# A residual term moved from an elementwise add into TensorE's sum, with a rewritten opening, in an edge-gated graph kernel

## The chip, the cores and the metric

The kernel runs on one core of one Trainium2 chip. The metric is the device time of one execution in microseconds (us). Of the kernel before there are three runs, with a median of 1230.34 us.

## What is computed

There are B = 16 batches of C = 1024 nodes with D = 256 features. Both `A_a` and `A_m` are the same sparse matrix `adj` (a few entries per row, and the diagonal).

```python
pre_u = einsum('bud,dk->buk', h_t, W1[:d]);  pre_v = einsum('bvd,dk->bvk', h_t, W1[d:])
hidden = relu(pre_u[:, :, None, :] + pre_v[:, None, :, :] + b1)
S = sigmoid(einsum('buvk,ko->buvo', hidden, W2)[..., 0] + b2[0])
a_t = einsum('buv,bud->bvd', S * A_a, h_t)
m_t = einsum('uv,bud->bvd', A_m, h_t) * h_t
z_t = beta1 * h_t + beta2 * (a_t @ Wa + ba) + beta3 * (m_t @ Wm + bm)
```

The change concerns the first term of the last line, `beta1 * h_t`. All of it is fp32.

## The kernel before, in words

**Blocks and steps.** The work is cut into 32 blocks: 4 groups of 4 batches (`GB`) times 8 tiles of 128 nodes. A block has 10 steps, so the main loop (L679) has 320 steps; s is the step within a block. In each step one list of 128 edges is handled. `fetch` (L450, POOL) gathers 128 rows of 8 KB from a table in DRAM: the left half of a row is pre_u, the right half is h. `expand` (L519, TensorE, two steps ahead) repeats the target rows pre_v into PSUM, in the two buffers `pc`. `gate` (L537) runs on VectorE: one add of table row and `pc` (L540), then four multiply-and-sum instructions (L544); then on ScalarE the sigmoid (L547) and four scalings (L550), followed by `left_adj` (L534) for the next step. `aggregate` (L552, TensorE, one step behind) sums the gathered h rows into PSUM by 32-column matmuls. Five gather buffers (`fetched`) are in turn.

**End of a block.** The sums are copied out (`half_end`, L569, ScalarE), transposed by TensorE and copied again by ScalarE (`turn_over`, L579 and L582), and half of them multiplied by hT on VectorE (`times_h`, L592). `block_end` (L597) forms the output in steps 3 to 6 of the next block: for each half of the batches a bias row (L382), then per batch two matmuls with `w_m` and two with `w_a` (L609), each with 128x128 stationary values and 256 moving columns, into a PSUM tile of two batches. In steps 5 and 7, after the gate of that step, VectorE does `h_blk = h_blk * beta1 + pz` (L613), where `h_blk` holds the rows of h, loaded from DRAM on SP's queue in the block's step 4 (L708). SP then writes `h_blk` out (L616). `tail` (L630) does the same in pieces for the last block.

**Other work between.** `rows` (L385) computes pre_u for the table of a group ahead of its use, `halves` (L403) pre_v of the next block. `load_hT` (L364, SP) loads transposed h for both, into a rotation of 10 buffers; a block's hT is freed after `times_h`. All small sums (`p`, `pl`, `pt`, `pz`) share two PSUM buffers, `misc`. `lists` (L241) is a generator in 11 pieces that makes the edge lists of one tile of nodes out of a loaded row block of adj (`key`); the heavy pieces are three maxima over 1024 columns on VectorE. Its calls are spread over the first 100 steps by the table `advance` (L660), and `fetch_val` gathers the edge values, on POOL.

**Order.** The kernel is scheduled by hand: each engine and each queue runs its instructions in the order in which the code issues them. `after(step, f)` puts a piece into a later step, where `do(n)` (L430, L694) issues it: after that step's gate and ahead of its `block_end`, `turn_over` and `halves`.

**The opening** (L458 to L501). POOL loads the keys of lists 0 to 3 (three of them into gather buffers) and clears the gather buffers. SP loads eight hT and copies rows of h into the table. Then a script of 15 strings orders `rows` (r), pieces of lists 0, 1 and 2 (digits), the value gathers (v), halves of block 0 (h) and the first five gathers (f). List 3 goes on in steps 4 to 17.

Of the kernel before, what the change touches and what calls it, by code (L numbers as in the profile page):

```python
# [13 lines left out]
P = 128  # L14
# [3 lines left out]
def kernel(  # L18
# [17 lines left out]
    out: bass.AP,  # L36
):


# [58 lines left out]

    w_u = load_weights(W1[0:D], "w_u")
    b1_b = load_rows(b1, D, "b1_b")  # L100
    w_v = load_weights(W1[D:2 * D], "w_v")
    w2_b = load_rows(W2, D, "w2_b")
# [4 lines left out]


    ones = fixed([P, 2], "ones")
    nc.vector.memset(ones[:, 0:1], 1.0)  # L110
# [71 lines left out]
    ident = fixed([P, P], "ident")  # L182
    nc.vector.tensor_scalar(ident, upto[:, :P], row, None, ALU.is_equal)
    place = upto[:, :W].rearrange("p (q v) -> p q v", v=V)
    slot, nth = upto, upto[:, :S]
# [11 lines left out]

    b1_p = fixed([P, D], "b1_p", FR)
    bias_p = fixed([P, D], "bias_p", FR)

# [14 lines left out]
    big = main.enter_context(tc.tile_pool(name="big", bufs=2))  # L215
    hts = main.enter_context(tc.tile_pool(name="hts", bufs=NT + 2))
    wk = main.enter_context(tc.tile_pool(name="wk", bufs=3))
# [8 lines left out]
    def aside(vt):  # L226
        return psc.tile([P, GD], FP, name="pc") if vt < EARLY else small("pl")

    NF = 5
    EARLY = 3
    fetched = []
    for i in range(NF):
        fetched.append(gat.tile([P, 2 * GD], FP, name=f"fetched{i}"))

    def clear(i):
        nc.gpsimd.memset(fetched[i][:, N if 1 <= i <= EARLY else 0:], 0.0)


    def lists(vt):  # L241
        key = fetched[vt + 1][:, :N] if vt < EARLY else big.tile([P, N], FP, name="key", bufs=1)
        nc.gpsimd.dma_start(key, adjT[vt * P:(vt + 1) * P, :])
        yield
# [124 lines left out]

    def copy_h(k, engine=nc.scalar):  # L370
        g, nt = k
        engine.dma_start(table[g][nt * P:(nt + 1) * P, GD:].rearrange("n (b d) -> n b d", b=GB),
                            x_rows[nt * P:(nt + 1) * P, g * GB:(g + 1) * GB, :])
# [29 lines left out]
    def halves(k):  # L403
# [13 lines left out]
        for h in range(2):  # L417
# [4 lines left out]
            for w in range(NW):  # L422
                s = slice((1 - w) * W, (2 - w) * W)
                nc.scalar.copy(X[s, w, c], pl[s])  # L424

    engines = mybir.EngineType
    main.enter_context(tc.manual_schedule(
# [13 lines left out]
    T = TW * NW  # L441

    BS = NG * NT

    def where(n):
        k, s = divmod(n, T)
        w, j = divmod(s, TW)
        return k, *order[k], w, j

    def fetch(n):  # L450
# [7 lines left out]
    made = [lists(vt) for vt in range(NT)]  # L458
    turn = [order[i] for i in (*range(2 * NT // 2, 3 * NT // 2), *range(NT // 2))]
    turn += [(1, vt) for _, vt in turn]  # L460
    for i in range(2):
        next(made[i])
    for i in range(NT):
        load_hT(turn[i])
    for i in range(NF):
        clear(i)
    for i in range(2, EARLY + 1):
        next(made[i])
    COPIES = 2
    for i in range(COPIES):  # L470
        copy_h(turn[i], nc.sync)

    script = ("r r 0 0", "r r 0", "r r 0 1", "0 r 1", "0 0 r r", "0 r 1", "r 0 0 v 1 r", "1 r 2 2", "1 1 r r h",
              "1 r h 2", "1 1 h 2", "2 f h h", "2 2", "2", "2 2")
    m = 0
    piece = None
    parts = halves(0)
    for t, turns_ in enumerate(script):
        step = t - 100
        do(step)  # L480
        for c in turns_.split():
            if c == "r":
                if m % 2 == 0:
                    piece = rows(turn[m // 2])
                    next(piece)
                go(piece, step)
                if m % 2 == 0 and m // 2 + COPIES < NT:
                    copy_h(turn[m // 2 + COPIES], nc.sync)
                m += 1
            elif c == "h":  # L490
                go(parts, step)
            elif c == "v":
                fetch_val(T)
                spread(b1_p, b1_b)
                next(parts)
            elif c == "f":
                for n in range(NF):
                    fetch(n)
            else:
                next(made[int(c)], None)  # L500
    do(len(script) - 100)  # L501

    def scale_late():
        nc.vector.tensor_scalar(ba_b, ba_b, be2, None, ALU.mult)
        nc.vector.scalar_tensor_tensor(bias, bias, be3, ba_b, ALU.mult, ALU.add)
        spread(bias_p, bias)
        nc.vector.tensor_scalar(w_a, w_a, be2, None, ALU.mult)
        nc.vector.tensor_scalar(w_m, w_m, be3, None, ALU.mult)

    marks, pcs, accs, evs, hbs, LTs, lefts = {}, {}, {}, {}, {}, {}, {}

# [56 lines left out]
    def turn_over(k, w, q, step):  # L571
# [18 lines left out]
        def times_h():  # L590
            m = LT[:, :, :, 0, v]
            nc.vector.tensor_tensor(m, m, hTs[order[k]].rearrange("p b c n -> p c b n")[:, :, :, v], ALU.mult)  # L592
            if w == NW - 1 and q == 1:
                del hTs[order[k]]
        after(step + 1, times_h)

    def block_end(k):  # L597

        g, vt = order[k]
        hb = hbs[k]  # L600
        for h in range(2):
            for bb in range(2):
                step = yield
                if bb == 0:
                    pz = small("pz")
                    add_row(pz, bias_p)
                for i, wt in enumerate((w_m, w_a)):
                    for c in range(DC):
                        nc.tensor.matmul(pz[:, bb * D:(bb + 1) * D], LTs[k][:, c, 2 * h + bb, i, :], wt[:, c, :],  # L609
                                         start=False, stop=(i == 1 and c == DC - 1), skip_group_check=True)  # L610

            def add(h=h, pz=pz):
                nc.vector.scalar_tensor_tensor(hb[:, 2 * h:2 * h + 2, :], hb[:, 2 * h:2 * h + 2, :], be1,  # L613
                                               pz.rearrange("p (b d) -> p b d", b=2), ALU.mult, ALU.add)
            after(step + 1, add)
        after(step + 2, lambda: nc.sync.dma_start(  # L616
            out[g * GB:(g + 1) * GB, vt * P:(vt + 1) * P, :].rearrange("b p d -> p b d"), hb))
        del hbs[k], LTs[k]

    tails = [(0, W, 0), (0, W, 1), (W, U, 2), (W + U, U, 3)]

    def tail_rows(t, v, m, f):
        g, vt = order[BS - 1]
        for i in range(P // m):
            b = g * GB + i + (f * P // m if m == W else 0)
            yield hbs[BS - 1][i * m:(i + 1) * m, f, :], t[b, vt * P + v:vt * P + v + m, :]

    def tail(parts, step):  # L630

        LT, hb = LTs[BS - 1], hbs[BS - 1]
        v, m, f = parts[0]
# [3 lines left out]
        nc.tensor.matmul(pz[:, :n], unit, bias_p.unsqueeze(1).to_broadcast([P, len(parts), D]),  # L637
                         start=True, stop=False, skip_group_check=True)
        for i, wt in enumerate((w_m, w_a)):
            for r in range(len(parts)):  # L640
# [8 lines left out]
        def add():  # L649
            z = hb[:, f:f + len(parts), :]  # L650
            nc.vector.scalar_tensor_tensor(z, z, be1, pz[:, :n].rearrange("p (r d) -> p r d", d=D), ALU.mult, ALU.add)  # L651
            for part in parts:
                for i, (z, o) in enumerate(tail_rows(out, *part)):
                    (nc.scalar if i % 2 else nc.sync).dma_start(o, z)
# [4 lines left out]

    advance = {}  # L660
    for i in range(EARLY, NT):
        for o in (0, 4, 5, 6, 7, 8, 9, 11, 13, 15, 17)[i == EARLY:]:
            advance[20 * (i - EARLY) + o] = (i,)
    loads = dict(zip((0, 1, 2, 6, 9, 13, 17, 23), turn[NT:]))
# [10 lines left out]
    for n in range(2):  # L675
        expand(n)
    left_adj(0)
    total = BS * T
    for n in range(total + 2):  # L679
# [15 lines left out]
        if n == 1:  # L695
# [7 lines left out]
            after(10, scale_late)  # L703
        if s == 4 and k < BS:
            hbs[k] = big.tile([P, GB, D], FP, name="h_blk")
            if k < BS - 1:
                g, vt = order[k]
                nc.sync.dma_start(hbs[k], x_rows[vt * P:(vt + 1) * P, g * GB:(g + 1) * GB, :])  # L708
            else:
                for v, m, f in tails:  # L710
                    for h, o in tail_rows(x, v, m, f):
                        nc.sync.dma_start(h, o)
        for i in advance.get(n, ()):
# [43 lines left out]
    do(total + 2)  # L757
    assert not due and not hTs and all(next(x, None) is None for x in made)
    main.close()
# [111 lines left out]
```

## Time and profile before

| | |
|---|---|
| median of three runs | 1230.34 us (1225.94 to 1235.77) |
| profiled execution, and its span | 1230.34 us, 1228.5 us |
| mean granted TensorE clock | 0.968 |
| first gate (L540) starts at | 89.16 us |
| blocks 0 to 9 (table of group 1, lists 2 to 7) | 89 to 491 us, 40.2 us each |
| blocks 10 to 14 (rows of group 2) | 491 to 655 us, 32.8 us each |
| blocks 15 and 16 (no rows) | 655 to 720 us, 32.5 us each |
| blocks 17 to 23 (rows of group 3) | 720 to 958 us, 34.0 us each |
| blocks 24 to 31 (no rows) | 958 to 1207 us, 31.1 us each |
| DMA moved | 393.5 MB, of which 31 loads of h_blk of 512 KB |

The starts of the blocks are those of every tenth L540. "Busy" of an engine is the time in which it has an instruction. TensorE overlaps its matmuls, and their ends are modelled, so its rate is read from the distance of starts. PEld is TensorE's loading of stationary values. A wait is put down to the instruction that came last by the profile.

### The profile page before, as it was taken

The numbers are of one execution on the slowest core, as the hardware profiler recorded it, in microseconds if no ns is written. First come the engines' busy times: TensorE is split into PE (matmuls) and PEld (weight loads), VectorE is DVE, ScalarE is ACT, GpSimd is POOL, SyncE is SP. The second block draws the span as 40 slices with busy tenths as digits, with TensorE's granted clock in tenths as the row PEclk, the third lists the DMA queues.
The fourth block names the chain that finished last, engine by engine and source line by source line (L and its number), as shares of the span: only waits on it lengthen the run. The fifth ranks groups of instructions, "written<-read, shape, count | busy, mean of one in ns | idle before, by whom it ended". The sixth has DMA issues, their size and how long they took to land. (4 is left out here: it accounts for less than half of the span.)

```text
span 1228.5 us, 23863 instructions
## 1 busy us (share of the span) xinstructions
PE 1108.6 (90%) x7697; PEld 723.5 (59%) x7697; DVE 1094.8 (89%) x3437; ACT 841.1 (68%) x2562; POOL 425.5 (35%) x419
## 2 busy tenths in 40 slices
PE   4767998997979989999999999999999999999996
PEld 3654665654546555666666556666666555665553
DVE  7659888999999899999899999889888999999994
ACT  1236675775656757777777777777777777777763
POOL 2227362362623614422333323222222333333330
PEclk8768999999999989999999999999999999999998
DMA  9569898898898989999999999999999988999992
GB/s 295 181 245 360 282 349 305 284 334 284 259 331 297 327 291 343 350 358 361 348 362 368 337 347 318 345 345 405 386 354 335 345 320 315 325 339 326 325 334 95
DMA packets 151975, 393.50 MB, mean 320 GB/s; under 512 B 16816, under 2 KB 110512, under 8 KB 115632
## 3 DMA queue, kind: packets, MB, share of 16 engines
q0 software_dynamic: 49792, 300.90, 66.4%
q1 hardware_dynamic: 85488, 76.03, 19.3%
q10 hardware_dynamic: 16560, 14.95, 3.7%
q8 instruction: 63, 1.03, 0.3%
q14 instruction: 72, 0.59, 0.1%
HBM read 395.88 MB, written 50.33 MB: 363 GB/s over the span
## 5 line engine op out<-in xcount | busy, mean ns | idle before, releaser
L452 POOL DMA_INDIRECT fetched<-table,uidx x320 | 329.9, 1031 | 705.0 <-PE acc L561 493.6
L544 DVE SCALAR_TENSOR_TENSOR t<-t,w_b 128x256 f32<-128x256 f32 x1280 | 469.9, 422 | 19.3 <-ACT X L412 0.5
L540 DVE TENSOR_TENSOR t<-fetched,pc 128x1024 f32<-128x1024 f32 x320 | 389.0, 1216 | 50.3 <-PE pc L524 25.2
L561 PE MATMUL acc<-fetched,left 128*32 128x256 f32 x4096 | 323.7, 392 | 26.9 <-ACT left L550 25.7
L550 ACT ACTIVATE left<-left,gt 128x32 f32<-128x32 f32 (+1 forms) x1280 | 299.4, 304 | 10.4
L524 PE MATMUL pc<-X,mark 128*128 128x512 f32 x640 | 247.3, 468 | 3.4 <-DVE t L540 1.9
L561 PEld LDWEIGHTS acc<-fetched,left 128*32 128x32 f32 x4096 | 122.7, 109 | 193.4 <-issue 68.0
L547 ACT ACTIVATE gt<-sc,b_b 128x4 f32<-128x4 f32 x320 | 95.4, 298 | 190.0 <-DVE t L544 189.5
L378 PE MATMUL misc<-w_u,hT 128*128 128x256 f32 x512 | 131.6, 406 | 23.5 <-ACT tab L394 12.9
L609 PE MATMUL misc<-w_m,LT 128*128 128x256 f32 x496 | 133.7, 392 | 0.0
L524 PEld LDWEIGHTS pc<-X,mark 128*128 128x128 f32 x640 | 118.4, 193 | 25.1 <-DVE LT L592 4.1
L609 PE MATMUL misc<-w_a,LT 128*128 128x256 f32 x496 | 127.3, 379 | 0.0
L378 PEld LDWEIGHTS misc<-w_u,hT 128*128 128x128 f32 x512 | 99.3, 202 | 45.1 <-ACT tab L394 14.4
L378 PE MATMUL misc<-w_v,hT 128*128 128x256 f32 x512 | 123.0, 384 | 0.0
L534 ACT ACTIVATE left<-onehot,val 128x128 f32<-128x128 bf16 (+1 forms) x320 | 116.6, 364 | 0.0
L609 PEld LDWEIGHTS misc<-w_m,LT 128*128 128x128 f32 x496 | 88.9, 189 | 34.8 <-issue 25.5
L336 POOL DMA_INDIRECT val<-in_adjT_dram,vidx x80 | 84.0, 1050 | 66.8 <-DVE b_p L194 40.0
L378 PEld LDWEIGHTS misc<-w_v,hT 128*128 128x128 f32 x512 | 98.5, 192 | 13.4
L544 DVE DVE_READ_ACCUMULATOR t<-t,w_b 128x1 f32 x1280 | 104.0, 81 | 0.0
L609 PEld LDWEIGHTS misc<-w_a,LT 128*128 128x128 f32 x496 | 94.2, 190 | 12.8
L569 ACT COPY ev<-acc 128x512 f32<-128x512 f32 x128 | 74.8, 585 | 28.9 <-PE acc L561 28.9
L424 ACT CAST X<-misc 64x512 fp32r<-64x512 f32 x128 | 74.3, 581 | 28.0 <-PE misc L421 23.9
(138 smaller groups left out, 860.1 us busy)
## 6 DMA issues: line engine op xcount, KB each, us to landing
hT<-in_xT_dram SPq DMA_DIRECT2D x40, 512.0 KB, 11.1
table<-tab SPq DMA_DIRECT2D x32, 512.0 KB, 5.2
h_blk<-in_x_dram SPq DMA_DIRECT2D x31, 512.0 KB, 13.4
out_dram<-h_blk SPq DMA_DIRECT2D x31, 512.0 KB, 5.5
table<-in_x_dram ACTq DMA_DIRECT2D x24, 512.0 KB, 11.8
fetched<-table,uidx POOLq DMA_INDIRECT x320, 7.9
table<-in_x_dram SPq DMA_DIRECT2D x8, 512.0 KB, 8.0
key<-in_adjT_dram POOLq DMA_DIRECT2D x5, 512.0 KB, 9.2
```

Source lines behind the costliest of these rows:

```text
L336: nc.gpsimd.indirect_dma_start(out=val[:, i, j:j + 1], out_offset=None, in_=adj_flat, in_offset=bass.IndirectOffsetOnAxis(ap=vidx[:, i, j: ...
L378: nc.tensor.matmul(p[:, bb * D:(bb + 1) * D], hT[:, 2 * h + bb, i, :], wt[:, i, :], start=(i == 0 and not begun), stop=(i == DC - 1), skip ...
L452: nc.gpsimd.indirect_dma_start(out=fetched[n % NF], out_offset=None, in_=table[g], in_offset=bass.IndirectOffsetOnAxis(ap=uidx[:, vt * NW ...
L524: nc.tensor.matmul(pcs[n][:, c], marks[n // TW][:, j * P:(j + 1) * P], cuts[k][:, w, c], start=True, stop=True)
L534: nc.scalar.activation(lefts[n][:, :m, :, 0, :], onehot[:, i, o:o + m, :].unsqueeze(2).to_broadcast([P, m, GB, V]), AF.Copy, scale=val[:, ...
L540: nc.vector.tensor_tensor(t, fetched[n % NF][:, :GD].rearrange("p (b d) -> p b d", b=GB), pcs.pop(n).rearrange("p (b d) -> p b d", b=GB), ...
L544: nc.vector.scalar_tensor_tensor(t[:, b, :], t[:, b, :], 0.0, w2_b, ALU.max, ALU.mult, accum_out=sc[:, b:b + 1])
L547: nc.scalar.activation(gt, sc, AF.Sigmoid, bias=b2_b)
L550: nc.scalar.activation(lefts[n][:, :m, b, 1, :], lefts[n][:, :m, b, 0, :], AF.Copy, scale=gt[:, b:b + 1])
L561: nc.tensor.matmul(accs[h][b * 2 * V:(b + 1) * 2 * V, r, :], left[:, i, b].rearrange("p k v -> p (k v)"), f[:, GD + b * D:GD + (b + 1) * D ...
L569: nc.scalar.copy(evs[q], accs.pop(q))
L609: nc.tensor.matmul(pz[:, bb * D:(bb + 1) * D], LTs[k][:, c, 2 * h + bb, i, :], wt[:, c, :], start=False, stop=(i == 1 and c == DC - 1), sk ...
```

## The change

The term beta1 h becomes two more matmuls per batch in `block_end`: stationary hT (128 features x 128 nodes), moving a 128x128 diagonal `diag` that holds beta1, made once. The finished sum is copied from PSUM by ScalarE into a new tile `z_blk` (one buffer), which SP writes out. Rows of h are no longer loaded. A block's hT is freed at the end of `block_end`, and the rotation has 11 buffers. The tail has the matmuls too, and VectorE copies its sums out.

The opening is another one. The keys of lists 0 and 1 are loaded first on SP, ahead of the eight hT; those of lists 2 and 3 on POOL in the opening's step 5; all into two `key` buffers. ScalarE, not POOL, clears the gather buffers. ScalarE's queue makes the eight copies into the table, each ahead of its `rows`. Ten steps replace the script: lists 0 and 1 advance in each, lists 2 and 3 by five pieces in steps 5 to 9 (in each step ahead of 0 and 1), two halves of `rows` per step. Value gathers come in step 9, the first five gathers after the opening; lists 2 and 3 end in steps 0 to 10 of the main loop. The spread of b1 is done before all lists.

```diff
+    diag = fixed([P, P], "diag")
+    spread(b1_p, b1_b)
-    hts = main.enter_context(tc.tile_pool(name="hts", bufs=NT + 2))
+    hts = main.enter_context(tc.tile_pool(name="hts", bufs=NT + 3))
-        key = fetched[vt + 1][:, :N] if vt < EARLY else big.tile([P, N], FP, name="key", bufs=1)
-        nc.gpsimd.dma_start(key, adjT[vt * P:(vt + 1) * P, :])
+        key = big.tile([P, N], FP, name="key", bufs=2)
+        (nc.sync if vt < 2 else nc.gpsimd).dma_start(key, adjT[vt * P:(vt + 1) * P, :])
+    def clear(i):
+        nc.scalar.copy(fetched[i], zero.to_broadcast([P, 2 * GD]))
...
+    for t in range(1, 11):
+        step = t - 100
+        do(step)
+        for i in (2, 3, 0, 1):
+            if i < 2 or 5 <= t < 10:
+                next(made[i], None)
+        while m < t * OP // 8 and m < OP:
+            if m % 2 == 0:
+                copy_h(turn[m // 2])
+                piece = rows(turn[m // 2])
+                next(piece)
+            go(piece, step)
+            if m % 3 == 0 and m // 3 < NF:
+                clear(m // 3)
+            m += 1
+        if t in (7, 8, 9, 10):
+            if t == 7:
+                parts = halves(0)
+                next(parts)
+            go(parts, step)
+            if t == 10:
+                go(parts, step)
+        if t == 9:
+            fetch_val(T)
...
+        nc.vector.tensor_scalar(diag, ident, be1, None, ALU.mult)
...
     def block_end(k):
         g, vt = order[k]
-        hb = hbs[k]
+        hT = hTs[order[k]]
+        zb = big.tile([P, GB, D], FP, name="z_blk", bufs=1)
...
                     add_row(pz, bias_p)
+                for c in range(DC):
+                    nc.tensor.matmul(pz[:, bb * D + c * P:bb * D + (c + 1) * P], hT[:, 2 * h + bb, c, :], diag,
+                                     start=False, stop=False, skip_group_check=True)
                 for i, wt in enumerate((w_m, w_a)):
...
             def add(h=h, pz=pz):
-                nc.vector.scalar_tensor_tensor(hb[:, 2 * h:2 * h + 2, :], hb[:, 2 * h:2 * h + 2, :], be1,
-                                               pz.rearrange("p (b d) -> p b d", b=2), ALU.mult, ALU.add)
+                nc.scalar.copy(zb[:, 2 * h:2 * h + 2, :].rearrange("p b d -> p (b d)"), pz)
             after(step + 1, add)
...
     def tail(parts, step):
...
+        for r in range(len(parts)):
+            for d in range(DC):
+                for b in range(c):
+                    nc.tensor.matmul(pz[b * m:(b + 1) * m, r * D + d * P:r * D + (d + 1) * P],
+                                     hT[:, r * c + b, d, v:v + m], diag, start=False, stop=False, skip_group_check=True)
...
-            z = hb[:, f:f + len(parts), :]
-            nc.vector.scalar_tensor_tensor(z, z, be1, pz[:, :n].rearrange("p (r d) -> p r d", d=D), ALU.mult, ALU.add)
+            nc.vector.tensor_copy(zs[0][:, f:f + len(parts), :].rearrange("p r d -> p (r d)"), pz[:, :n])
...
+    advance = {0: (2,), 1: (2, 3), 2: (3,), 3: (2,), 4: (3,), 5: (2,), 6: (3,), 7: (2,), 8: (3,), 9: (2,), 10: (3,)}
+    for i in range(4, NT):
...
-                nc.sync.dma_start(hbs[k], x_rows[vt * P:(vt + 1) * P, g * GB:(g + 1) * GB, :])
```

More of the change, by code (lines that the diff above doesn't have):

```diff
@@ L99 @@
     w_u = load_weights(W1[0:D], "w_u")
+    w_v = load_weights(W1[D:2 * D], "w_v")
     b1_b = load_rows(b1, D, "b1_b")
-    w_v = load_weights(W1[D:2 * D], "w_v")
     w2_b = load_rows(W2, D, "w2_b")
@@ L106, in fixed @@
         return const.tile(shape, dt, name=name)
+    zero = fixed([P, 1], "zero")
+    nc.vector.memset(zero, 0.0)
     ones = fixed([P, 2], "ones")
@@ L226, in aside @@
     def aside(vt):
[L227 to L238, printed above, removed]
+        return psc.tile([P, GD], FP, name="pc") if vt < 2 else small("pl")
     def lists(vt):
-        key = fetched[vt + 1][:, :N] if vt < EARLY else big.tile([P, N], FP, name="key", bufs=1)
-        nc.gpsimd.dma_start(key, adjT[vt * P:(vt + 1) * P, :])
+        key = big.tile([P, N], FP, name="key", bufs=2)
+        (nc.sync if vt < 2 else nc.gpsimd).dma_start(key, adjT[vt * P:(vt + 1) * P, :])
         yield
@@ L368, in load_hT, with copy_h @@
                           xT_rows[:, g * GB * DC:(g + 1) * GB * DC, nt * P:(nt + 1) * P])
-    def copy_h(k, engine=nc.scalar):
+    def copy_h(k):
         g, nt = k
-        engine.dma_start(table[g][nt * P:(nt + 1) * P, GD:].rearrange("n (b d) -> n b d", b=GB),
+        nc.scalar.dma_start(table[g][nt * P:(nt + 1) * P, GD:].rearrange("n (b d) -> n b d", b=GB),
                             x_rows[nt * P:(nt + 1) * P, g * GB:(g + 1) * GB, :])
@@ L424, in halves @@
                 nc.scalar.copy(X[s, w, c], pl[s])
+    NF = 5
+    fetched = []
+    for i in range(NF):
+        fetched.append(gat.tile([P, 2 * GD], FP, name=f"fetched{i}"))
+    def clear(i):
+        nc.scalar.copy(fetched[i], zero.to_broadcast([P, 2 * GD]))
     engines = mybir.EngineType
@@ L441, with scale_late @@
     T = TW * NW
+    made = [lists(vt) for vt in range(NT)]
+    for i in range(2):
+        next(made[i])
+    turn = [order[i] for i in (*range(2 * NT // 2, 3 * NT // 2), *range(NT // 2))]
+    turn += [(1, vt) for _, vt in turn]
+    for i in range(NT):
+        load_hT(turn[i])
+    OP = 2 * NT
+    m = 0
+    piece = parts = None
+    for t in range(1, 11):
[22 more added lines that the diff above has]
+            fetch_val(T)
+    do(11 - 100)
+    def scale_late():
+        nc.vector.tensor_scalar(ba_b, ba_b, be2, None, ALU.mult)
+        nc.vector.scalar_tensor_tensor(bias, bias, be3, ba_b, ALU.mult, ALU.add)
+        spread(bias_p, bias)
+        nc.vector.tensor_scalar(w_a, w_a, be2, None, ALU.mult)
+        nc.vector.tensor_scalar(w_m, w_m, be3, None, ALU.mult)
+        nc.vector.tensor_scalar(diag, ident, be1, None, ALU.mult)
     BS = NG * NT
@@ L448, in where @@
         return k, *order[k], w, j
+    marks, pcs, accs, evs, LTs, lefts = {}, {}, {}, {}, {}, {}
     def fetch(n):
@@ L455, in fetch @@
             bounds_check=N - 1, oob_is_err=False)
[L458 to L513, printed above, removed]
     def load_mark(q):
@@ L592, in times_h @@
             nc.vector.tensor_tensor(m, m, hTs[order[k]].rearrange("p b c n -> p c b n")[:, :, :, v], ALU.mult)
-            if w == NW - 1 and q == 1:
-                del hTs[order[k]]
         after(step + 1, times_h)
@@ L612, in add @@
             def add(h=h, pz=pz):
-                nc.vector.scalar_tensor_tensor(hb[:, 2 * h:2 * h + 2, :], hb[:, 2 * h:2 * h + 2, :], be1,
-                                               pz.rearrange("p (b d) -> p b d", b=2), ALU.mult, ALU.add)
+                nc.scalar.copy(zb[:, 2 * h:2 * h + 2, :].rearrange("p b d -> p (b d)"), pz)
             after(step + 1, add)
         after(step + 2, lambda: nc.sync.dma_start(
-            out[g * GB:(g + 1) * GB, vt * P:(vt + 1) * P, :].rearrange("b p d -> p b d"), hb))
-        del hbs[k], LTs[k]
+            out[g * GB:(g + 1) * GB, vt * P:(vt + 1) * P, :].rearrange("b p d -> p b d"), zb))
+        del hTs[order[k]], LTs[k]
     tails = [(0, W, 0), (0, W, 1), (W, U, 2), (W + U, U, 3)]
+    zs = []
     def tail_rows(t, v, m, f):
@@ L627, in tail_rows @@
             b = g * GB + i + (f * P // m if m == W else 0)
-            yield hbs[BS - 1][i * m:(i + 1) * m, f, :], t[b, vt * P + v:vt * P + v + m, :]
+            yield zs[0][i * m:(i + 1) * m, f, :], t[b, vt * P + v:vt * P + v + m, :]
     def tail(parts, step):
-        LT, hb = LTs[BS - 1], hbs[BS - 1]
+        LT, hT = LTs[BS - 1], hTs[order[BS - 1]]
+        if not zs:
+            zs.append(big.tile([P, GB, D], FP, name="z_blk", bufs=1))
         v, m, f = parts[0]
@@ L655, in tail @@
         after(step + 1, add)
[L660 to L663, printed above, removed]
+    advance = {0: (2,), 1: (2, 3), 2: (3,), 3: (2,), 4: (3,), 5: (2,), 6: (3,), 7: (2,), 8: (3,), 9: (2,), 10: (3,)}
+    for i in range(4, NT):
+        for o in (0, 4, 5, 6, 7, 8, 9, 11, 13, 15, 17):
+            advance[20 * (i - 3) + o] = (i,)
     loads = dict(zip((0, 1, 2, 6, 9, 13, 17, 23), turn[NT:]))
@@ L676 @@
         expand(n)
+    for n in range(NF):
+        fetch(n)
     left_adj(0)
@@ L703 @@
             after(10, scale_late)
[L704 to L707, printed above, removed]
-                nc.sync.dma_start(hbs[k], x_rows[vt * P:(vt + 1) * P, g * GB:(g + 1) * GB, :])
[L709 to L712, printed above, removed]
         for i in advance.get(n, ()):
@@ L757 @@
     do(total + 2)
-    assert not due and not hTs and all(next(x, None) is None for x in made)
+    assert not due and len(hTs) == 1 and all(next(x, None) is None for x in made)
     main.close()
```

## The prediction

> **What bounds the kernel now.** I read the page's busy shares first, then busy time block by block, then TensorE's and VectorE's own waits, and the order of time in one block where they disagree.
>
> ```profile
> PE 1108.6 (90%) x7697; PEld 723.5 (59%) x7697; DVE 1094.8 (89%) x3437; ACT 841.1 (68%) x2562; POOL 425.5 (35%) x419
> ```
>
> Two engines are nearly full, so the average decides nothing. The windows by block (busy of PE, PEld, DVE, ACT, POOL, then clock and DMA share) show stages:
>
> ```profile
> 253.50:293.70 40.20, 34.42 (x237) 20.89 (x235) 39.13 (x117) 27.19 (x86) 16.86 (x16) 0.96 0.84 305
> 623.00:655.00 32.00, 31.54 (x231) 20.77 (x226) 29.77 (x96) 25.18 (x79) 10.09 (x10) 1.00 1.00 374
> 853.00:891.00 38.00, 37.76 (x263) 25.79 (x266) 30.95 (x99) 27.86 (x84) 9.92 (x10) 1.00 1.02 386
> 1053.00:1085.00 32.00, 30.69 (x226) 19.02 (x220) 30.51 (x101) 24.66 (x78) 10.23 (x10) 1.00 0.90 324
> ```
>
> Stage A, blocks 0 to 9: VectorE is full from block 4 on (39.1 of 40.2 us), because it makes the lists; in blocks 1 to 3 TensorE carries the rows of group 1 and is nearly as full. Stage B, the 12 blocks with rows (10 to 14, 17 to 23): TensorE is full. Stage C, the 10 others (15, 16, 24 to 31): both are at 30.5 to 30.7 of 32. TensorE's waits from 500 to 1200 us are small:
>
> ```profile
> PE acc L561 <- ACT left L550: 12.0, 22, 1.5
> PE misc L421 <- ACT LT L582: 7.5, 21, 0.8
> ```
>
> That is about 1 us of some 33 per block. What TensorE gains in work in stage B is paid in time.
>
> **What the Trainium skill says.** "TensorE: Matmul & The Clock Gate", section "LDWEIGHTS (loading the stationary operand)", prices a load by its columns over 1.2 GHz, 107 ns for 128. The trace agrees: ten fp32 matmuls with 128x128 stationary values and only 58 moving columns (first row below) start (1.32 - 0.275) / 9 = 0.116 us apart, 0.275 being the length of one. The same page ("Architectural detail: the array is 16× 32×32, not 1× 128×128") calls ScalarE a strict FIFO, so a copy put there waits behind the scalings of its step; the rows further below agree. "SBUF — State Buffer", "Who interferes with whom", says that VectorE and GpSimd exclude each other on a shared port pair; here L116 took 5.69 us beside POOL's clears (2.57 to 8.83 us), and L283, of the same shape without them, 0.545.
>
> **The change part by part.**
>
> ```profile
> 146.26 1.32 PE L302 MATMUL misc<-RR,made 128*128 128x58 f32 x10
> L609 PE MATMUL misc<-w_m,LT 128*128 128x256 f32 x496 | 133.7, 392 | 0.0
> L569 ACT COPY ev<-acc 128x512 f32<-128x512 f32 x128 | 74.8, 585 | 28.9 <-PE acc L561 28.9
> L613 DVE SCALAR_TENSOR_TENSOR h_blk<-h_blk,be,misc 128x512 f32<-128x512 f32 x62 | 46.0, 742 | 1.1 <-PE misc L609 1.1
> ```
>
> *TensorE.* 8 matmuls per block, 128x128 stationary and 128 moving columns, fp32. No such ordinary matmul is in the trace. Lower end: 0.116 us, where the load sets the distance; the transposes L579, of the same size, are as close (8 in 1.09 us). Upper end: as L609 with 256 columns, 4 in 1.03 us, (1.03 - 0.392) / 3 = 0.213. L609 at 256 columns and L302 at 58 fit a load that hides 128 columns, so I take 0.116: 0.93 us per block. The upper end is 1.70.
>
> *VectorE.* Two L613 leave each block: the next instruction starts 0.67 us later, so 1.34 us per block.
>
> *ScalarE.* Two copies of 128x512 from PSUM at 0.585 (L569): 1.17 us per block. It is busy 25 of 32 us, so this is hidden by its waits for the gates, except in step 7. There it is a hand-over. Before, from one block in stage C:
>
> ```profile
> 1074.43 0.81 PE L524 MATMUL pc<-X,mark 128*128 128x512 f32 x2
> 1075.46 1.22 DVE L540 TENSOR_TENSOR t<-fetched,pc 128x1024 f32<-128x1024 f32 x1
> ...
> 1078.18 0.74 DVE L613 SCALAR_TENSOR_TENSOR h_blk<-h_blk,be,misc 128x512 f32<-128x512 f32 x1
> 1078.29 0.30 ACT L547 ACTIVATE gt<-sc,b_b 128x4 f32<-128x4 f32 x1 [0.68 <-DVE t L544]
> 1079.14 1.09 PE L579 MATMUL misc<-ident,ev 128*128 128x128 f32 x8
> 1079.49 0.38 ACT L534 ACTIVATE left<-onehot,val 128x128 f32<-128x128 bf16 x1
> 1079.83 0.59 ACT L582 COPY LT<-misc 128x512 f32<-128x512 f32 x1
> ```
>
> VectorE frees the PSUM buffer of `pz` by 1078.9, before the transposes ask for it. In ScalarE's order the copy comes after L534, 1079.83 to 1080.4, so the second four transposes wait for it, and the LT copies, the next use of `misc` (L421) and `expand` behind them in TensorE's queue come later. In stage B the same rows at 919 us give: first four transposes end near 919.9 with the added matmuls, copy ends 920.4, so some 0.5 us; half of it falls into the 0.47 us that TensorE waits there already for LT. I charge 0.25 us. The step-5 copy frees its buffer long before step 7.
>
> *Stage B:* 12 x (0.93 + 0.25) = +14.2 us. VectorE's gain is worth nothing there.
>
> *Stage C:* from steps 2 to 7 TensorE runs without a pause; `expand` ends at 1075.24 and the gate that needs it starts at 1075.46: 0.22 us of slack. With 0.7 us of added matmuls ahead of it that gate is late by about 0.5, and it is TensorE, not the removed L613, that sets it. After the hand-over the gate of step 9, at 1082.14 before, comes at about 1082.8: +0.66. 10 x 0.66 = +6.6 us.
>
> *Stage A:* blocks 0 to 3, half of the 0.93: 4 x 0.47 = +1.9. Blocks 4 to 9: VectorE is full and TensorE has 3 to 8 us of slack, so the 1.34 counts, less about 0.3 for later hand-overs: 6 x -1.0 = -6.0 us.
>
> *DMA and queues.* 31 loads of 0.5 MB leave SP's queue, 4% of the bytes. All L540 together waited 17.6 us for gathers, mostly where TensorE was behind: I take 0, at best -5. The hT of a block is freed four steps later, but with 11 buffers each tight load (steps 93 to 143, 223) finds a buffer freed 7 steps before instead of 1: no new wait. `z_blk` has one buffer: written out in step 8, landing in 5.5 us (the writes before), needed again 7 steps on, some 22 us: hidden. `diag`, 0.28 us once, is nothing.
>
> *Opening.* Before:
>
> ```profile
> 3.50 5.69 DVE L116 TENSOR_SCALAR upto<-ukey 128x640 f32<-128x640 f32 x1
> 34.21 1.07 ACT L394 COPY tab<-misc 128x512 f32<-128x512 f32 x2 [17.54 <-DMA table<-tab]
> 89.16 1.21 DVE L540 TENSOR_TENSOR t<-fetched,pc 128x1024 f32<-128x1024 f32 x1
> ```
>
> Afterwards POOL clears nothing: L116 gains 5.1 us, and the spread of b1 (0.28 + 0.42 + 0.35) comes first, so lists start at 12.8 - 5.1 + 1.05 = 8.8 us. Heavy pieces of lists 0 and 1: 2 x (1.21 + 3 x 1.23 + 2 x 1.28) = 15, to 24. Keys 2 and 3 wait on POOL for these buffers and land 9.2 us later, 33. Another 15 us of heavy pieces and some 12 of light ones and waits for ScalarE give the indices of list 0 at about 60. Ten value gathers at 1.3: 73. The first gather lands 7.9 later, 81 to 82, and a first gate at about 85 with something for ScalarE. Its queue holds five clears of about 2.1 us (twice L250's 1.04 for half the columns), eight copy issues of 0.56 and the table's copies, where it stood for 17.5 us before. The two keys ahead of hT on SP cost two issues of 2.5 us (eight took 19.83). These can make the first gate 78 at best, 95 at worst. I take -4.
>
> *Tail.* 8 small matmuls in each of three pieces, at the rate of L644's, some 0.06: +0.7 on the last two pieces.
>
> Sum: 14.2 + 6.6 + 1.9 - 6.0 - 4 + 0.7 = +13.4. The profiled execution took 1230.34 us (span 1228.5 and 1.9 around it), which is also the median: **1244 us**, its own range 1234 to 1254.
>
> **Rivals.**
>
> *VectorE sets the pace in A and C.* Place: the gate of step 7. If `expand` is there first in spite of the added matmuls (distance under about 0.06 us, or the block's TensorE run starting earlier once VectorE is), the removed 1.34 us counts in A and C, -13 each, and B pays about 0.3 per block after TensorE's own waits close: 1230 - 26 - 4 + 4 = 1204. For it: VectorE is as full as TensorE in C. Against: the slack of 0.22 us, and TensorE's unbroken run.
>
> *The added matmul costs 0.21, not 0.116.* B +9, C +8, blocks 0 to 3 +2: 1263. For it: no ordinary 128-column matmul is measured. Against: L302.
>
> *The opening loses.* ScalarE in its order, behind clears and table copies, is late with the list's pieces, and the first gate comes at 93: 1252. For it: the 17.54 us wait. Against: VectorE's 5 us.
>
> That the h loads cannot matter is likely: their landing (13.4 us) was hidden behind a block.
>
> **How the numbers follow.** About 1% is what a measurement of this kernel can tell from no change: 1218 to 1243. Forecast: 0.60 (slower 0.30, same 0.29, faster 0.01). Costly matmul: 0.17 (slower 0.15, same 0.02). VectorE's pace: 0.14 (faster 0.10, same 0.04: a half of it gives 1224). Opening: 0.09 (slower 0.05, same 0.03, faster 0.01). Faster 0.12, same 0.38, slower 0.50. The range 1217 to 1266 takes in the costly matmul and half of VectorE's case; what is below or above is less than 2 in 10.
>
> **What would show it.** Right: blocks 10 to 23 longer by about 1.2 us, 24 to 31 by 0.7, 4 to 9 shorter by 1; a group of two added matmuls in 0.23 us of starts; L579 waiting for ScalarE's new copy in step 7; first gate near 85 us. Wrong: blocks 24 to 31 shorter than 30.5 us (VectorE's pace), added matmuls 0.2 apart, or a first gate outside 78 to 95.

## The result and the profile after

The kernel after took 1264.28 us (median of four runs, 1263.52 to 1267.30), against 1229.18 us for the kernel before (four runs). The ratio is 1.0283, with a 95% interval of 1.0237 to 1.0330: slower. The forecast was 1244 us. Its direction was right and its size was not: about 35 us were lost where 14 were expected.

The profiled execution of after took 1263.99 us (span 1262.0), so the two traces differ by 33.5 us. The page's first part, for after:

```profile
PE 1158.1 (92%) x8241; PEld 773.5 (61%) x8241; DVE 1054.5 (84%) x3377; ACT 882.9 (70%) x2629; POOL 414.9 (33%) x412
```

VectorE lost 40 us of work, as intended, and ScalarE gained 42. TensorE has 544 more records than before (8241 - 7697). The change adds 8 calls in each of 31 blocks, which is 248, and 24 in the tail, together 272: half of 544. Four of the groups by line say why, for after:

```profile
L607 PE MATMUL misc<-w_m,LT 128*128 128x256 f32 x496 | 127.6, 380 | 0.0
L603 PE MATMUL misc<-diag,hT 128*128 128x128 f32 x496 | 81.7, 287 | 0.0
L611 ACT COPY z_blk<-misc 128x512 f32<-128x512 f32 x62 | 34.9, 562 | 0.0
L575 PE MATMUL misc<-ident,ev 128*128 128x128 f32 x512 | 84.8, 290 | 14.7 <-ACT z_blk L611 13.8
```

L603 is the added matmul. 31 blocks of 8 calls would be x248; the trace has x496. Each fp32 matmul of the code is two instructions on TensorE, each with a weight load of its own. The row of L607 beside it says the same: x496 for 31 blocks of 8 calls with `w_m`. That row stood in the profile of before (as L609, x496), and the prediction quoted it. Two kinds of matmul are one record for each call: those on fp32r values (the 320 x 2 calls of `expand` are x640), and the transposes (L575: 32 blocks of 16 calls, x512).

What they cost is in the order of time. TensorE in one block of the last stage, after (start, length, instruction):

```profile
1094.42 0.50 PE L376 MATMUL misc<-bias_p,unit 128*128 128x512 f32 x1
1094.76 0.61 PE L603 MATMUL misc<-diag,hT 128*128 128x128 f32 x4
1095.20 1.03 PE L607 MATMUL misc<-w_m,LT 128*128 128x256 f32 x4
...
1098.49 0.71 PE L603 MATMUL misc<-diag,hT 128*128 128x128 f32 x4
1099.04 0.81 PE L607 MATMUL misc<-w_m,LT 128*128 128x256 f32 x3
```

Each group of two calls is x4. The first takes 0.44 us from its start to the next start, 0.11 for one instruction: the distance that the prediction took (0.116), and close to the estimate of 107 ns that the formula of the Trainium skill ("TensorE: Matmul & The Clock Gate", "LDWEIGHTS (loading the stationary operand)") gives for loading 128 columns. What agrees is the distance of starts; the trace's own records of these loads are 0.19 us long on average. The second takes 0.55: it follows the 32-column matmuls of `aggregate`, where the first follows the bias row. A block has two of each: 2 x (0.44 + 0.55) = 1.98 us, where the prediction had 0.93.

The windows by block (busy of PE, PEld, DVE, ACT, POOL, then clock and DMA share), for after, the same four stages as in the prediction:

```profile
259.40:298.70 39.30, 34.74 (x252) 22.45 (x246) 37.89 (x115) 28.07 (x87) 16.41 (x16) 0.91 0.81 294
637.60:671.90 34.30, 34.03 (x251) 22.79 (x250) 29.17 (x95) 26.64 (x81) 10.10 (x10) 1.00 0.94 332
877.50:917.50 40.00, 39.59 (x282) 27.32 (x274) 29.53 (x95) 28.50 (x84) 9.92 (x10) 1.00 0.95 329
1082.40:1114.00 31.60, 29.91 (x217) 19.29 (x214) 27.00 (x87) 23.71 (x73) 9.51 (x10) 1.00 0.83 282
```

In the last two stages VectorE, once 30.5 to 31, is down to 27 to 29.5 with no gain in time: it now waits. Its largest wait from 500 to 1200 us (total, times, longest) is that of the gate for `expand`, before and after:

```profile
DVE t L540 <- PE pc L524: 17.3, 18, 2.1
DVE t L536 <- PE pc L520: 66.2, 82, 2.9
```

The work taken from VectorE has turned into waiting for TensorE.

Taken between the starts of the blocks (every tenth gate), the traces differ as follows (us):

| stretch | before | after | measured | predicted |
|---|---|---|---|---|
| to the first gate | 89.2 | 93.4 | +4.3 | -4 |
| blocks 0 to 3 | 164.3 | 166.1 | +1.8 | +1.9 |
| blocks 4 to 9 | 237.6 | 237.7 | +0.1 | -6.0 |
| stage B: 10 to 14, 17 to 23 | 402.4 | 419.0 | +16.6 | +14.2 |
| stage C: 15, 16, 24 to 31 | 313.7 | 324.8 | +11.1 | +6.6 |
| after the last gate | 21.4 | 21.0 | -0.4 | +0.7 |

### The profile page after: what moved, and what is told of

Its sections match the earlier page's. It is cut to its first block, busy times and chain, and to the rows that moved or that the text cites. A ratio compares the mean times of both kernels' runs of the same rounds, so it can differ in the third digit from the quotient of the medians.

```text
span 1262.0 us, 24904 instructions
## 1 busy us (share of the span) xinstructions
PE 1158.1 (92%) x8241; PEld 773.5 (61%) x8241; DVE 1054.5 (84%) x3377; ACT 882.9 (70%) x2629; POOL 414.9 (33%) x412
## 3 DMA queue, kind: packets, MB, share of 16 engines
q1 hardware_dynamic: 64480, 56.11, 14.4%
## 5 line engine op out<-in xcount | busy, mean ns | idle before, releaser
L557 PE MATMUL acc<-fetched,left 128*32 128x256 f32 x4096 | 314.2, 392 | 18.4 <-ACT left L546 18.2
L557 PEld LDWEIGHTS acc<-fetched,left 128*32 128x32 f32 x4096 | 115.7, 109 | 180.7 <-issue 56.2
L607 PE MATMUL misc<-w_m,LT 128*128 128x256 f32 x496 | 127.6, 380 | 0.0
L607 PE MATMUL misc<-w_a,LT 128*128 128x256 f32 x496 | 127.3, 379 | 0.0
L607 PEld LDWEIGHTS misc<-w_a,LT 128*128 128x128 f32 x496 | 94.2, 190 | 12.8
L575 PE MATMUL misc<-ident,ev 128*128 128x128 f32 x512 | 84.8, 290 | 14.7 <-ACT z_blk L611 13.8
```

What stands on the lines that cost most here:

```text
L557: nc.tensor.matmul(accs[h][b * 2 * V:(b + 1) * 2 * V, r, :], left[:, i, b].rearrange("p k v -> p (k v)"), f[:, GD + b * D:GD + (b + 1) * D ...
L575: nc.tensor.transpose(pt[:, i * P:(i + 1) * P], ev[:, r, c * P:(c + 1) * P], ident)
```

## The experiments

There are fifteen runs of nine kernels, in four sets. The kernels of one set share a chip and the runs of the kernel before. From set to set the kernel before took 1233.5, 1249.1, 1232.9 and 1244.8 us, so everything below is given as its ratio to the kernel before of its own set. Times of blocks come from one profiled execution of each kernel.

Theory: the added matmuls are 16 instructions and not 8 per block, and TensorE's time is the loss. Rivals: the hand-over to ScalarE, the opening, and the dropped loads of h or VectorE's relief.

### How much of the term: none, half, twice

**None:** the added matmuls of a block are left out (those of the tail stay), all else is after.

```diff
-                for c in range(DC):
-                    nc.tensor.matmul(pz[...], hT[:, 2 * h + bb, c, :], diag, start=False, stop=False, ...)
```

> The changed kernel without the added matmuls in block_end (the tail keeps them): the term beta1 h is left out of the output in all blocks but the last. Theory 'instructions' (each added fp32 matmul of the code is two instructions on TensorE, 16 per block and not 8, 1.98 us of starts per block, and most of the loss is that): 1233 us, between 1227 and 1240, with blocks 10 to 31 back at the length they had before or up to 0.3 us above, and the first gate still near 93 us. Rival 'hand-over' (the copy in ScalarE's order in step 7, ahead of the transposes, is the loss): stays above 1250. Rival 'opening' (the loss is made ahead of and in the blocks with lists): stays above 1250 with blocks 10 to 31 unchanged against the changed kernel.

Measured: 1232.71 us, ratio 1.0003 (0.9982 to 1.0025). Without the matmuls nothing is left of the loss in sum, and nothing is gained either, although VectorE is relieved of 1.34 us per block. By stage it is not all zero: the first gate is at 95.0 us (89.2 before), stage B takes 403.3 us (402.4 before) and stage C 310.2 (313.7). So in stage C 3.5 us came back of the 13.4 that VectorE was spared there, in stage B none.

**Half:** only the first of each pair of batches has the term, 8 instructions per block, which is what the prediction counted.

```diff
-                for c in range(DC):
+                for c in range(DC if bb == 0 else 0):
```

> The changed kernel with the added matmuls for one batch of each pair only (8 TensorE instructions per block instead of 16; beta1 h is left out for every second batch). This is the amount of TensorE work that the prediction had counted. Theory 'instructions': half-way between no added matmuls and the changed kernel, 1246 to 1252 us, and less if the first part of the added work falls into waits that TensorE had. Rival 'hand-over': within 4 us of the changed kernel.

Measured: 1249.27 us, ratio 1.0132 (1.0085 to 1.0180). On 1229.18 that is 1245 us, near the forecast of 1244. The close agreement is partly luck: against before, stages B and C are 9.1 and 3.6 us longer, where 14.2 and 6.6 were forecast, and what is missing there was lost ahead of the first gate (+3.0, forecast -4) and in blocks 4 to 9 (+0.4, forecast -6).

**Twice:** each added matmul is followed by one with a diagonal of zeros, 32 instructions per block.

```diff
+                    nc.tensor.matmul(pz[...], hT[:, 2 * h + bb, c, :], nil, start=False, stop=False, ...)
```

> The changed kernel with each added matmul followed by one more with a diagonal of zeros (32 TensorE instructions per block instead of 16, the output is the same). Theory 'instructions': TensorE has nothing left to hide the second 1.8 to 2.0 us in, so the step is larger than that from none to the changed kernel: 1264 + 31 x 1.9 = 1323, at least 1310. Rival 'hand-over': the copy comes to wait less as TensorE gets later, so under 1300.

Measured: 1303.56 us, ratio 1.0575 (1.0530 to 1.0619), less than the 1310 that were expected at least, and above the 1300 of the rival. TensorE's order of time in this kernel:

```profile
1090.66 0.38 PE L605 MATMUL misc<-diag,hT 128*128 128x128 f32 x2
1090.88 0.39 PE L607 MATMUL misc<-nil,hT 128*128 128x128 f32 x2
1091.10 0.39 PE L605 MATMUL misc<-diag,hT 128*128 128x128 f32 x2
```

Every call, again, is x2, and takes 0.22 us. The second set adds 8 x 0.22 = 1.78 us of starts per block.

What the three show together: in the 22 blocks from 10 on, 8 instructions (0.88 us at 0.11) cost 15.3 us or 0.70 per block; 32 (some 3.76 us, 1.98 + 1.78) cost 63.7 us or 2.89. So 77 to 80% of what is added to TensorE is paid. The rest can have gone into waits that TensorE had. Its waits from 500 to 1200 us in the kernel with no added matmuls:

```profile
PE misc L575 <- ACT z_blk L608: 10.0, 21, 0.8
PE acc L557 <- ACT left L546: 9.0, 16, 1.0
PE misc L376 <- ACT X L418: 6.0, 21, 0.8
```

and in after:

```profile
PE acc L557 <- ACT left L546: 5.9, 13, 1.3
PE misc L376 <- ACT X L418: 4.8, 21, 0.2
PE misc L575 <- ACT z_blk L611: 1.3, 2, 1.1
```

25.0 us of waits have become 12.0. In both lists the line of L575 on `z_blk` is the hand-over of step 7.

### Who moves the sums out

**VectorE copies:** after, with the sums moved out by VectorE.

```diff
-                nc.scalar.copy(zb[...], pz)
+                nc.vector.tensor_copy(zb[...], pz)
```

> The changed kernel with the finished sums copied out by VectorE, in the place where VectorE stood before, instead of ScalarE. Theory 'instructions': the matmuls stay, so it stays within 8 us of 1264 (1256 to 1270): the hand-over (transposes wait for the copy 20.8 us in all by the loads' waits, 13.8 by the matmuls') is given back, VectorE's 1.3 us per block is taken again. Rival 'hand-over': back to 1240 or below.

Measured: 1268.43 us, ratio 1.0288 (1.0244 to 1.0333), as after (1.0283). Neither a cost nor a gain of the move to ScalarE shows.

**VectorE copies and no matmuls:** both edits above.

> The changed kernel without the added matmuls (beta1 h is left out in all blocks but the last) and with the sums copied out by VectorE. With ScalarE's copy this kernel took as long as the kernel before, though VectorE had 1.3 us per block less to do. If the hand-over to ScalarE ate that gain, this one, which takes VectorE's time again and gives the hand-over back, is as long: 1228 to 1236 at 1233. If TensorE alone set the pace and neither counts, it is the same as well; the waits tell the two apart: under the first, the transposes' wait for the copy (10.0 us from 500 to 1200 us) goes to under 2 and VectorE's waits for the repeated rows (26.6) go under 20.

Measured: 1258.53 us, ratio 1.0111 (1.0066 to 1.0157). Against the 1.0003 of the kernel with no matmuls this looked like a gain of 1% from VectorE's relief. But the two had run on different chips. So all four corners of the square were run on one chip:

**No matmuls, ScalarE copies.**

> Added matmuls 0, copy by ScalarE (beta1 h left out in all blocks but the last), again, so that all four of the square {0, 16 added TensorE instructions per block} x {ScalarE, VectorE copies the sums} stand on one chip. If VectorE's time is worth something only while TensorE is not loaded: ratio to the kernel before 0.998 to 1.003, and 0.7 to 1.2% under its partner with VectorE. If the earlier difference of the partners was one between chips: within 0.4% of its partner.

**No matmuls, VectorE copies.**

> Added matmuls 0, copy by VectorE (beta1 h left out in all blocks but the last). Ratio 1.007 to 1.014 if VectorE's 1.3 us per block counts when TensorE is not loaded; 1.000 to 1.004 if the earlier difference was one between chips.

**Matmuls, ScalarE copies** (after itself).

> The changed kernel as it is, on the chip of the other three. Ratio 1.026 to 1.032.

**Matmuls, VectorE copies.**

> The changed kernel with the copy by VectorE. With TensorE loaded VectorE's time is worth nothing: ratio within 0.4% of the changed kernel, 1.025 to 1.033.

Measured (ratio, interval, us):

| | ScalarE copies | VectorE copies |
|---|---|---|
| no matmuls | 0.9987 (0.9962 to 1.0012), 1231.77 | 1.0002 (0.9981 to 1.0022), 1234.64 |
| matmuls | 1.0261 (1.0220 to 1.0301), 1265.03 | 1.0279 (1.0230 to 1.0328), 1268.42 |

The 1% was a difference between chips: the kernel with no matmuls and VectorE's copy stood at 1.0111 and here at 1.0002, and on a third chip (below) at 1.0029, each time against the kernel before on the same chip. Even a ratio of this kind holds only to about 1% from chip to chip. The three traces of that one kernel say where: blocks 0 to 9 took 428.7, 399.3 and 416.1 us in them, blocks 10 to 31 (to the last gate) 711.8, 716.7 and 717.6. Why the chips differ in the first stage was not settled.

The copy's engine is worth 0.15 to 0.18%, with intervals that overlap widely: not told apart from nothing. The matmuls cost 33.3 us (1265.03 - 1231.77) where ScalarE copies and 33.8 where VectorE does. In the 22 blocks from 10 on they cost 31.1 us, 1.41 per block of the 1.98 added, 71%.

### The opening and the term, each alone

**The term only:** before, with the new end of a block, the new tail, the diagonal and no loads of h; the opening stays the old one.

> The new beta1 term (added matmuls, copy on ScalarE, no loads of h, 11 hT buffers) in the kernel before, whose opening and list plan stay. Theory 'instructions': the opening is a small part, so nearly all of the loss stays: ratio to the kernel before 1.022 to 1.028 (1256 to 1264 at 1229), first gate at 89 us. Rival 'opening': ratio below 1.012.

Measured: 1273.0 us, ratio 1.0216 (1.0166 to 1.0266), just below what was expected.

**The opening only:** after, with the old end of a block, the old tail and the loads of h.

> The new opening and list plan with the old end of a block (VectorE's add, loads of h, 10 hT buffers). Theory 'instructions': first gate at 93 to 95 us instead of 89, some of it given back in the first blocks, where list 3 asks for less: ratio 1.000 to 1.005. Rival 'opening': ratio 1.015 or more.

Measured: 1258.11 us, ratio 1.0072 (1.0031 to 1.0113), more than was expected.

With the sum of the parts still open, both ran again on another chip, with the kernel that isolates the loads:

> The new opening and list plan with the old end of a block, again. If the opening costs what its later first gate says (4 us): ratio 1.003 to 1.008. If it costs nothing over the first blocks: 0.998 to 1.002.

> The new beta1 term in the kernel before with its old opening, again. If the added TensorE instructions are all of the loss: ratio 1.024 to 1.029, as far above the kernel before as the changed kernel. If the opening has a share: 1.019 to 1.023.

> The new opening, no added matmuls, no loads of h, VectorE copies the sums (beta1 h left out in all blocks but the last). Same as the opening alone within 0.3% if the loads of h are hidden; 0.5% or more below it if dropping them gives time back.

Measured: opening alone 1251.98 us, ratio 1.0066 (1.0045 to 1.0087); term alone 1269.4 us, 1.0190 (1.0137 to 1.0242); new opening, no matmuls, VectorE copies, no loads of h 1246.76 us, 1.0029 (1.0005 to 1.0053). The opening costs 0.7%, measured on two chips. The last kernel has the opening too and stands 0.37% below the opening alone, between the two limits that were set for it, so it doesn't decide whether dropping the loads of h (with a one-input copy in place of the add on VectorE) gives time back. Nor do the same two kernels on the chip of the first pair: there they took 1258.53 and 1258.11 us, with no gain.

The ledger, in per cent: matmuls +2.7 (1.0261 - 0.9987), opening +0.7, loads dropped 0 to -0.4, copy on ScalarE 0 to -0.15; sum 2.85 to 3.4, for a measured 2.6 (in the square) and 2.8. For the term alone, 2.15 to 2.7, for a measured 1.90 and 2.16. The parts come from different chips; those under half a per cent are not resolved, and only the matmuls are large against that.

### Another way to relieve TensorE

Before, without its bias row in the sum: ScalarE multiplies the rows of h by beta1, GpSimd adds the bias row, and VectorE's last step is a plain add.

```diff
-                    add_row(pz, bias_p)
...
+            nc.scalar.activation(hbs[k - 1], hbs[k - 1], AF.Copy, scale=be1)
+            nc.gpsimd.tensor_tensor(hbs[k - 1], hbs[k - 1], bias.unsqueeze(1).to_broadcast([P, GB, D]), ALU.add)
```

> The kernel before with less TensorE work, where the change gave more: the bias row, one matmul of 512 columns for each half of a block (0.34 us of starts each, 0.68 per block), is no longer a product. ScalarE multiplies the loaded rows of h by beta1 and GpSimd adds the bias row to them ahead of need; VectorE then adds rows and sum. Theory 'instructions': in blocks 10 to 31 about 0.7 of TensorE's time is paid, so 0.5 us per block back, 22 x 0.5 = 11: 1218 to 1224 at 1229 if GpSimd's add does not hold up VectorE; its cost is not measured yet, and with one long hold per block the gain is gone. Rival 'hand-over' and rival 'opening': no change.

Measured: 1321.89 us, ratio 1.0601 (1.0568 to 1.0633), a large miss. Two lines from the groups of this kernel (the last column: idle time ahead of them, and what ended it):

```profile
L592 DVE TENSOR_TENSOR LT<-LT,hT 128x512 f32<-128x512 f32 (+1 forms) x65 | 87.8, 1351 | 23.9 <-ACT LT L582 23.8
L716 POOL TENSOR_TENSOR h_blk<-h_blk,bias 128x1024 f32<-128x1024 f32 x31 | 74.4, 2401 | 69.5 <-ACT h_blk L715 60.7 <-ACT left L550 8.9
```

Two things at once. VectorE's multiply of LT, untouched by the edit, took 678 ns on average before and 1351 here. The average mixes two kinds: 24 of the 65 overlap an add of GpSimd (2.4 us each) and took 2.5 us, the other 41 took 0.67 as before. The Trainium skill states it ("SBUF — State Buffer", "Who interferes with whom"): a VectorE instruction with two SBUF inputs contends with a GpSimd instruction that reads SBUF. The trace agrees. And GpSimd stood 60.7 us waiting for ScalarE's multiply, with the gathers of the next gates queued behind it. The two causes were not taken apart. The expectation had named the hold of VectorE as a risk; whether the relief of TensorE is worth anything by itself stays open.

## Why the prediction was right or wrong

**The step that failed: the count in the TensorE term.** "8 matmuls per block" at 0.116 us gave 0.93. The duration was right (0.11 by the starts), and the count was that of calls in the code: such an fp32 call is two instructions, so it is 16 and 1.98 us. The distance of 0.116 had been taken per record of the trace and multiplied by calls of the code. Two rows that the prediction quoted held the answer: L609 is x496 for 248 calls, and the "ten fp32 matmuls" of L302 are five calls. The third row that it leaned on, the transposes, has one record per call and so hid the doubling. Taking the matmuls out, on one chip and with nothing else changed, took 33.3 us off with ScalarE's copy and 33.8 with VectorE's, and the loss grows with their number.

**"What TensorE gains in work in stage B is paid in time":** three quarters right. Of the 1.98 us, 1.41 were paid; TensorE's waits for ScalarE shrank by about the rest (13.0 us over some 21 blocks, 0.6 each). With the count mended and all else kept, the prediction's sum would be 12 x (1.98 + 0.25) = 26.8 for B, 10 x (0.66 + 1.05) = 17.1 for C, 4.0 for blocks 0 to 3, and the other terms as they were: +38.6, or 1269 us, where 1264 were measured. That this is near owes something to luck too: the time to the first gate and blocks 4 to 9 came out 14.4 us above their terms, the other stages 19.5 below theirs. The terms that were off besides the count:

- **Blocks 4 to 9, -6 predicted, +0.1 measured.** VectorE's 1.34 us were not recovered there even with no added matmuls (+0.2 and +0.4 us over the six blocks in the kernels with none and with half). VectorE's idle time in those blocks rose instead, from 15 us of 238 to 23 in after and 24 with no matmuls; in after it waited 8.0 us for gathers and 6.0 for `expand` there. It was full, but its pace depended on these too: a busy engine is not one whose work is all on the path.
- **The hand-over, +0.25 per block in stage B predicted, nothing measured.** The wait exists where TensorE comes early: from 500 to 1200 us the transposes waited 10.0 us in 21 times in the kernel with no matmuls, and 8.9 us in 21 times in the one with half of them, which has the TensorE work that the prediction counted: 0.42 us each, near its 0.5. With the full work TensorE comes later. In after the transposes waited 1.3 us in two times, and their weight loads (PEld) 5.6 us in 20 times. One of these loads, the times at the left in us, in the timeline of after:

```profile
1109.89 1.29 PE L575 MATMUL misc<-ident,ev 128*128 128x128 f32 x8
1109.91 0.56 ACT L611 COPY z_blk<-misc 128x512 f32<-128x512 f32 x1
1110.53 0.42 PEld L575 LDWEIGHTS misc<-ident,ev 128*128 128x128 f32 x4 [0.21 <-ACT z_blk L611]
```

  The copy ends at 1110.47 and the second four loads start at 1110.53, after a wait of 0.21 us; the eight transposes run on without a break. Copying on VectorE leaves no such wait in these blocks and gives no time back: in the square blocks 10 to 31 take 743.3 us so, and 744.1 with ScalarE's copy. In blocks 0 to 9 the hand-over does show, with 12.5 of the 13.8 us that the row of L575 above has in all, in 4 times. VectorE's copy leaves 8.1 us in 4 times there, and the blocks are no shorter (407.7 us, 400.4 with ScalarE's, on one chip).
- **The opening, -4 predicted, +4.3 to the first gate and +0.7% in all measured.** This was the rival "the opening loses", which put the first gate at 93. The timeline of after:

```profile
3.52 0.49 DVE L119 TENSOR_SCALAR upto<-ukey 128x640 f32<-128x640 f32 x1
...
31.80 1.23 DVE L243 SCALAR_TENSOR_TENSOR key<-key,ukey 128x1024 f32<-128x1024 f32 x1 [7.07 <-DMA key<-in_adjT_dram]
...
74.53 1.07 POOL L330 DMA_INDIRECT val<-in_adjT_dram,vidx  x1 [49.29 <-DVE eq L306]
...
87.71 1.00 POOL L506 DMA_INDIRECT fetched<-table,uidx  x1 [0.30 <-issue]
...
93.44 1.22 DVE L536 TENSOR_TENSOR t<-fetched,pc 128x1024 f32<-128x1024 f32 x1 [16.76 <-DMA fetched<-table,uidx]
```

  L119 took 0.49 us instead of 5.69, so the 5 us of relief from GpSimd's clears came as predicted. So did the wait of 7.07 us for key 2, which the prediction had landing at 33. What it had too small is what comes next, from key 2 to the indices of list 0: VectorE's waits from 31 to 75 us, besides those for the loads of keys:

```profile
DVE low L407 <- ACT X L406: 7.2, 2, 3.7
DVE from L264 <- PE pc L259: 4.3, 1, 4.3
DVE key L249 <- ACT unread L244: 3.0, 1, 3.0
```

  These 14.5 us, 10.2 of them for ScalarE, come to the distance from the 60 of the prediction to the 74.5 at which GpSimd could begin the value gathers. After that the chain is as predicted: ten gathers at 1.3 us, first row gather at 87.7, first gate 5.7 us later. The opening alone costs 8 us (0.66% of 1244.8), of which some 4 lie before the first gate. Where the others lie was not settled. The traces point to blocks 0 to 9: with the opening alone these took 426 and 422 us on the two chips, at a mean granted clock of 0.93 and 0.91; with the term alone and the old opening 410 and 415 us, at 0.97 and 0.95.

**Stage C:** the mechanism held. In the ten blocks of stage C in after, the gate of step 7 waited for `expand` 10.9 us in 10 times, and those of steps 6 and 8 another 12.4; before, step 7 had no such wait. The size follows the count.

**The loads of h, "0, at best -5":** 5 us less on one chip (0.37%), nothing on another; within what was allowed, and not settled.

**The rivals.** VectorE setting the pace (1204) asked for 13 us in stage A and 13 in stage C. Even with no matmuls stage C gave back 3.5 us (3.9 in the second run of that kernel) and blocks 4 to 9 none (+0.2 and +1.4), so VectorE's work did not set the pace. The ratio of 1.0003 alone would not show this, since that kernel also has the opening's loss. The costly matmul (0.21, 1263) gave nearly the measured time for the wrong reason: the cost of a call was twice the forecast, but as two instructions of 0.11. The rival asked what one instruction costs, and not how many there are.

**Open:** whether ScalarE's copy is better than VectorE's (0.15 to 0.18%, within the noise), what the dropped loads of h are worth, the opening's second half, and why the kernel before differs by 1.6% between chips.

## What to carry to other kernels

Before a duration from the trace is multiplied by a count, take the count from the trace too: divide the x of a row like the one to be added by the calls that the code makes. When work leaves an engine that looks full, ask whether the other full engine has slack in the same stage, since the 30 to 36 us of copies that ScalarE took off VectorE in the square changed the time by no more than the runs can tell (0.15 to 0.18%). A half and a double dose of a suspected cost show more than taking it away alone: whether the price grows with the dose. Compare small effects on one chip, because an effect of 1% that showed between two chips was gone when both kernels ran on one; and compare them by stage, because a total that meets the forecast can be a sum of misses, as that of the half dose was.

## What the runs showed of the hardware

- An fp32 matmul is two TensorE instructions with two weight loads (x496 for 248 calls); an fp32r one (x640 for 640 calls) and an fp32 transpose (x512 for 512 calls) are a single instruction. With 128x128 stationary and 128 moving columns one fp32 call takes 0.22 us in a row of its like.
- Moving 128x512 fp32 from PSUM to SBUF took 0.562 us on ScalarE and 0.685 on VectorE (no matmuls, VectorE copies).
- A VectorE multiply of 128x512 fp32 with both inputs in SBUF takes 0.68 us; where it overlapped a GpSimd add of 128x1024 fp32, which itself takes 2.4 us, it took 2.5 us.
